# Reordering the last half block of a four-layer kernel: where the block ahead is finished, and who multiplies the last half's factors

## The chip, the cores and the metric

The kernel runs on one core of one Trainium2 chip. The metric is device time in microseconds (us) of one execution. A core has four computing engines, each with its own instruction queue worked in order: PE (TensorE, matrix products, results in PSUM), DVE (VectorE), ACT (ScalarE) and POOL (GpSimd); SP (SyncE) here only issues DMAs. Before the change three runs took 1389.89, 1390.21 and 1393.8 us, median 1390.21.

## What is computed

Eight stages one after the other on a residual x of 8 x 512 rows of 128 values in float32: for each of four layers an attention-like part and a feed-forward part, each behind a layer norm and added to x. The change touches the last one, in which both operands of every product are rounded to a 4-bit grid by blocks of 16:

```python
def fp4_quant_dequant(x):
    """Blockwise FP4 (E2M1) quantize + dequantize along the last dim."""
    shape = x.shape
    xb = x.reshape(shape[:-1] + (shape[-1] // BLOCK, BLOCK))
    scale = jnp.max(jnp.abs(xb), axis=-1, keepdims=True) / 6.0
    scale = jnp.maximum(scale, jnp.float32(1e-12))
    xn = xb / scale
    idx = jnp.searchsorted(_MID, jnp.abs(xn))
    q = _GRID[idx] * jnp.sign(xn) * scale
    return q.reshape(shape)
...
gate = fp4_linear(x, w_gate)
y = fp4_linear(x, w_up)
h = jax.nn.silu(gate) * y
return fp4_linear(h, w_down)
```

Here x has 128 columns and h has 352. fp4_linear rounds both operands so and multiplies them. The stage ahead of it in the same layer is a causal filter of 21 taps along the rows.

## The kernel before, in words

The eight batches of 512 rows ("blocks") go through the last two layers in frames: a loop over frames runs the attention of the layer before, and hooks in it call steps of the last layer for earlier blocks. The last frames have no attention left to hide behind. For them the function `end()` (line 2358) writes the order out by hand; the tile framework keeps it on each engine and sets the waits between engines from what each instruction reads and writes. Three things are interleaved there: **L**, the feed-forward of the block before the last (four tiles of 128 rows), and **A** and **B**, the two halves of the last block (two tiles each: 0 and 1, 2 and 3). The steps, with their lines:

- `quant_x1`, `quant_x2`, `turn_x` (2101): round the normalized x (VectorE, the last multiple on GpSimd), turn it on PE, copy it on ACT.
- `gated(j, at_end, thirds)` (2115) and `gate_out` (2127): two products of 352 columns (line 250, the helper of all products) into a pair of PSUM banks; tanh on ACT (2131). With `thirds` also a copy of the second product on ACT (2134). `gated_v` (2147) runs the rest: (tanh + 1) x gate on VectorE (2137), then the factor that makes h: with `thirds` on GpSimd, from SBUF (2139), else on VectorE, from PSUM (2141). Before the change L is called without `thirds`, A and B with.
- `quant_h1` (2154) calls `fp4_scale` (1363): maxima of the blocks of 16 (reduction, 1374), reciprocals (1376, 1377), scale (GpSimd, 1378), normalized values (1379). `quant_h2` calls `fp4_round` (1382): mask the exponent (1391), maximum and multiple (1394), add (1395), subtract (1396) on VectorE, then the multiple by the scale on GpSimd (1397), for two tiles at once (704 values a partition). `quant_h2_tile` (2160) does it for one tile (352).
- `turn_h` (2183): per tile three transposes on PE (2189) and a copy on ACT (2192). `down` (2196): three products a tile, then `added` (2072; line 2073), the sum into x on VectorE, and `stored` (2211; line 2212), the DMA of the result.
- `keep_clock(n)` (814): n products of the identity with itself, whose result nobody reads; they only keep PE working.

A float32 product of this kernel shows as two passes (records) in the trace, a transpose as one. PSUM banks named "one" go round in pairs: whoever takes the third waits until the first has been read. So B's first turned tile takes the bank of A's products. The buffers of the scale, of the normalized values and of the masks exist once for each size.

Of the kernel before, what the change touches and what calls it, by code (L numbers as in the profile page):

```python
# [17 lines left out]
F32 = mybir.dt.float32  # L18
I32 = mybir.dt.int32
U32 = mybir.dt.uint32  # L20
AF = mybir.ActivationFunctionType
ALU = mybir.AluOpType
# [3 lines left out]
P = 128  # L26
# [138 lines left out]
def body(ctx, tc, dram, spans, x_in, ib, it, ic, ei, out):  # L165
    nc = tc.nc
# [22 lines left out]
    def bank(tag="one"):  # L189
        if tag == "one" and "own" in banks:  # L190
            return banks["own"]
        return banks["pool"].tile([P, TB], F32, tag=tag, name="ps1", bufs=banks["tags"][tag])
# [5 lines left out]
    def load(blob, engine, pool=const):  # L198
        rows, cols = dram[blob].shape
        t = pool.tile([rows, cols], F32, tag=f"blob_{blob}", name=f"blob_{blob}")  # L200
        engine.dma_start(t, dram[blob])
        return {k: t[:, lo:hi] for k, (lo, hi) in spans[blob].items()}

    x = [resid.tile([P, J, D], F32, tag=f"x{b}", name=f"x{b}") for b in range(NB)]
    c = load("c", nc.scalar)
# [43 lines left out]
    def mm(out_, lhs, rhs, start=True, stop=True):  # L249
        nc.tensor.matmul(out_, lhs, rhs, start=start, stop=stop)  # L250
# [25 lines left out]
    def cols(t, j):  # L276
        return t[:, j * P : (j + 1) * P]
# [536 lines left out]
    def keep_clock(n):  # L814

        ps = bank()
        for _ in range(n):
            mm(cols(ps, 0), ident, ident)
# [563 lines left out]
    def fp4_round(pool, dst, sc, a, blocks, room=None):  # L1382

        shape = [P, blocks, 16]
        room = room or blocks
        m = pool.tile([P, room, 16], F32, tag=f"fm{room}", name="fm")[:, :blocks, :]  # L1390
        nc.vector.tensor_scalar(
            m.bitcast(I32), a.bitcast(I32), 0x7F800000, None, ALU.bitwise_and
        )
        nc.vector.tensor_scalar(m, m, 1.0, 1.5 * 2.0**22, ALU.max, ALU.mult)
        nc.vector.tensor_tensor(a, a, m, ALU.add)  # L1395
        nc.vector.tensor_tensor(a, a, m, ALU.subtract)
        nc.gpsimd.tensor_tensor(
            dst.rearrange("p (n k) -> p n k", k=16),
            a,
            sc.unsqueeze(2).to_broadcast(shape),  # L1400
            ALU.mult,
        )
# [3 lines left out]
    def late():  # L1406
# [11 lines left out]
        with tc.tile_pool(name="a2", bufs=2) as wp, tc.tile_pool(name="l3", bufs=1) as lp:  # L1418
# [253 lines left out]
            def context(n):  # L1672
                ex, sm, vs = exs.pop(n)
                ps = bank("c")
                for kt in range(J):
                    for i in range(2):
                        mm(
                            ps[64 * i : 64 * (i + 1), :],
                            vs[:, kt, i, :],
                            ex[kt][:, i, :],  # L1680
                            start=(kt == 0),
                            stop=(kt == J - 1),
                        )
                ct = wp.tile([P, TB], F32, tag="ct", name="ct")
                nc.scalar.copy(ct, ps)
                return ct

            def output(n, ct):
                b, cc = divmod(n, 8)
                if cc == 0:  # L1690
                    outs[b] = bank("o")
                for j in range(J):
                    mm(
                        cols(outs[b], j),
                        cols(ct, j),
                        cols(a2["l"], cc),
                        start=(cc == 0 and j == 0),
                        stop=(cc == 7 and j == J - 1),
                    )
                if cc == 7 and n < N - 1:  # L1700
                    add_to_residual(b, outs[b].rearrange("p (j d) -> p j d", j=J))
# [284 lines left out]
            def shared3(b):  # L1986

                t = {}

                def xp():  # L1990
                    if "xp" not in t:
                        t["xp"] = lp.tile([P, pad + TB], F32, tag="xp", name="xp", bufs=2)
                        nc.gpsimd.memset(t["xp"][:, :pad], 0.0)
                    return t["xp"]

                def tile_(name, make):
                    if name not in t:
                        t[name] = make()
                    return t[name]

                return xp, tile_

            def layer3(b, xp, tile_, part=(0, J), conv_bank="one", h_tag="h"):
# [4 lines left out]
                n = hi - lo  # L2008
# [63 lines left out]
                def added(ps):  # L2072
                    nc.vector.tensor_tensor(
                        x[b][:, j0:j1, :],
                        x[b][:, j0:j1, :],
                        ps[:, lo:hi].rearrange("p (j d) -> p j d", d=D),
                        ALU.add,
                    )
# [78 lines left out]
                def quant_h2(i):  # L2157
                    fp4_round(lp, pair(i), *t["fh", i], 44)

                def quant_h2_tile(i, j):  # L2160
                    sc, a = t["fh", i]
                    k = slice(22 * j, 22 * (j + 1))
                    h = tile_("h", h_tile)
                    fp4_round(lp, h[:, 2 * i + j, :], sc[:, k], a[:, k, :], 22)

                def blocks_h(i):
                    m = lp.tile([P, 44, 16], F32, tag="fm44", name="hb")
# [26 lines left out]
                        )  # L2194

                def down():
                    ht = tile_("ht", None)
                    po = bank()
                    for j in range(j0, j1):
                        for k, _ in thirds:  # L2200
                            mm(
                                cols(po, j),
                                ht[:C3, j, k, :],
                                wt["down"][:C3, k, :],
                                start=(j == j0 and k == 0),
                                stop=(j == j1 - 1 and k == 2),
                            )
                    added(po)
                    stored()

                def stored():
                    nc.sync.dma_start(
                        out[b * TB + lo : b * TB + hi, :].rearrange("(j p) d -> p j d", p=P),
                        x[b][:, j0:j1, :],
                    )
# [107 lines left out]
            for b in range(1, NB):  # L2323
                stats, scale, turn_, t_ = norm_steps(b, new_xt(b), "lb")
                n = {1: 3, 2: 5, 3: 14, 4: 26, 5: 33, 6: 40, 7: 47}[b]
# [32 lines left out]
            def end():  # L2358

                xp, tile_ = shared3(NB - 1)  # L2360
                A, B = (
                    layer3(NB - 1, xp, tile_, (2 * i, 2 * i + 2), "co"[i], "ge") for i in range(2)
                )
                L = last
                f = start[NB - 2]
                for key in [k for k in steps if k[0] >= f + 8]:
                    del steps[key]
                ct = context(N - 1)
                output(N - 1, ct)
                for h in (A, B):  # L2370
                    h.added(outs[NB - 1])
                    h.stats()
                L.gated(0, True, False)
                L.gated(1, True, False)
                A.scale()
                A.turn_()
                L.gated_v(0)
                B.scale()
                L.gated(2, True, False)
                L.gated_v(1)  # L2380
                B.turn_()
                L.gated(3, True, False)
                A.conv_tile(0)
                A.conv_tile(1)
                L.quant_h1(0)
                L.gated_v(2)
                L.quant_h2(0)
                L.gated_v(3)
                L.quant_h1(1)
                A.conv_added()  # L2390
                A.stats2()
                L.turn_h(0)
                L.quant_h2(1)
                B.conv_tile(2)
                B.conv_tile(3)
                A.scale2()
                A.quant_x1()
                A.quant_x2()
                B.conv_added()
                B.stats2()  # L2400
                A.turn_x()
                A.gated(0, True)
                B.scale2()
                A.gated(1, True)
                L.turn_h(1)
                A.gated_v(0)
                B.quant_x1()
                A.gated_v(1)
                B.quant_x2()
                L.down()  # L2410
                keep_clock(6)
                B.turn_x()
                B.gated(2, True)
                B.gated(3, True)
                A.quant_h1(0)
                A.quant_h2(0)
                B.gated_v(2)
                B.gated_v(3)
                keep_clock(8)
                B.quant_h1(1)  # L2420
                A.turn_h(0)
                B.quant_h2_tile(1, 0)
                B.quant_h2_tile(1, 1)
                A.down()
                keep_clock(22)
                B.turn_h(1)
                B.down()

# [290 lines left out]
```

## Time and profile before

| | us |
|---|---|
| median of three runs | 1390.21 |
| the profiled execution, its own time | 1394.63 |
| its span, first to last instruction | 1392.8 |
| L's sum into x (line 2073, 128x512) starts | 1369.92 |
| A's rounding: reduction starts / last subtraction starts | 1370.53 / 1375.10 |
| A's multiple on GpSimd (line 1397) starts | 1376.14 |
| B's gate factors on GpSimd (line 2139) | 1377.48 to 1379.29 |
| B's rounding: reduction starts / last subtraction starts | 1379.33 / 1385.51 |
| A's sum into x / B's sum into x start | 1385.95 / 1389.24 |
| last DMA issue (line 2212) starts | 1389.69 |

Times within the span count from the first instruction. Over the whole span PE is busy for 95%, DVE and ACT for 73% each, POOL for 46%; these shares say little about the last 30 us, which are read instruction by instruction. In a row of the timeline stand the start, the length, the engine, the line and the tiles written and read (`h<-fa,fsc`), and in brackets how long the engine had been idle and whose result ended that.

### The profile page before, as it was taken

To read this page: it belongs to the slowest core of one execution; us is meant where nothing else is said; L and a number is where in the kernel's file an instruction comes from. 1 tells how busy PE (TensorE), PEld (TensorE's weight loads), DVE (VectorE), ACT (ScalarE), POOL (GpSimd) and SP (SyncE) were. 2 spreads that over 40 slices of the span, in tenths; PEclk is the share of its full clock that TensorE was granted. 3 is DMA by queue.
4 is the path that set the end of the run, shared out by engine and by line. 5 is a ranking of instruction groups with operands and counts; after the bars stand their busy time and mean duration, and the time that the engine had idled before them with its cause. 6 is when DMAs were issued, how large, how long until landed. Compare 5 with 4: busy or idle time off the path is not lost.

```text
span 1392.8 us, 33124 instructions
## 1 busy us (share of the span) xinstructions
PE 1325.6 (95%) x12918; PEld 705.9 (51%) x12918; DVE 1013.9 (73%) x2149; ACT 1013.0 (73%) x2058; POOL 642.5 (46%) x749
## 2 busy tenths in 40 slices
PE   7889999999989999999999999999999999999997
PEld 3662222222267655547447545555555555555576
DVE  5786556666467778863783778888788797887876
ACT  6869999999978566665684686786767767667632
POOL 5655666666632533330472354353443634424432
PEclk9999999999999999999999999999999999999999
DMA  5019999999681011241211101101011010110000
GB/s 180 1 27 133 137 127 127 133 129 135 87 272 31 28 40 35 55 123 30 61 31 38 44 2 22 29 3 33 20 22 23 9 33 20 18 27 9 2 9 16
DMA packets 110845, 80.28 MB, mean 58 GB/s; under 512 B 61728, under 2 KB 103456, under 8 KB 106337
## 3 DMA queue, kind: packets, MB, share of 16 engines
q1 hardware_dynamic: 108959, 74.23, 29.0%
q0 software_dynamic: 1152, 2.36, 0.6%
q8 instruction: 102, 1.67, 0.5%
q10 hardware_dynamic: 578, 1.57, 0.3%
q14 instruction: 54, 0.44, 0.1%
HBM read 60.09 MB, written 18.04 MB: 56 GB/s over the span
## 4 chain that ended last, share of the span: by engine, by line
PE 50%; ACT 23%; DVE 20%; issue 3%; POOL 2%; DMA 1%; SPq 0%; DVEq 0%; ACTq 0%; POOLq 0%
PE ps L250 40%; PE ps L1571 8%; ACT hm L570 6%; ACT ex L1650 6%; DVE nm L1644 5%; ACT hm L569 3%; ACT prod L2038 2%; DVE acc L2024 1%; PE ps L2221 1%; DVE fa L1395 1%; DVE s L732 1%; DVE fa L1379 1%; ACT h L389 1%; DVE fsc L1374 1%; ACT q L1532 1%
## 5 line engine op out<-in xcount | busy, mean ns | idle before, releaser
L1650 ACT ACTIVATE ex<-ps,nm 128x512 f32<-128x512 f32 x512 | 345.2, 687 | 174.5 <-DVE nm L1644 166.2
L1644 DVE TENSOR_REDUCE nm<-ps 128x2 f32<-128x1024 f32 x256 | 301.1, 1210 | 39.2 <-PE ps L250 39.0
L250 PE MATMUL ps<-q,k 64*64 64x512 f32 (+1 forms) x2240 | 258.4, 564 | 9.1 <-ACT ex L1650 7.1
L250 PE MATMUL ps<-ex,vs 128*64 128x512 f32 x1024 | 233.8, 598 | 1.3 <-DVE sm L1664 1.1
L1665 POOL TENSOR_TENSOR vs<-v,sm 128x256 f32<-128x256 f32 x128 | 78.4, 613 | 294.4 <-DVE sm L1664 270.6
L588 POOL TENSOR_TENSOR acc<-acc,pr 128x512 f32<-128x512 f32 x119 | 165.5, 1391 | 93.8 <-DVE pr L582 85.8
L1571 PE MATMUL ps<-xt,blob_a 64*64 64x512 f32 x912 | 207.8, 589 | 0.1
L570 ACT ACTIVATE hm<-ps,blob_f 128x1536 f32<-128x1536 f32 x128 | 196.2, 1533 | 0.0
L582 DVE SCALAR_TENSOR_TENSOR pr<-ps,blob_f,gs 128x512 f32<-128x512 f32 x120 | 90.0, 750 | 93.6 <-PE ps L250 72.2
L250 PEld LDWEIGHTS ps<-q,k 64*64 64x64 f32 x2240 | 74.7, 132 | 152.4 <-ACT ex L1650 78.3
L250 PE MATMUL ps<-h,w 32*128 32x512 f32 x1024 | 147.4, 639 | 1.1 <-ACT hm L569 0.6
L250 PEld LDWEIGHTS ps<-ex,vs 128*64 128x64 f32 x1024 | 68.4, 136 | 152.9 <-issue 129.7
L250 PE MATMUL ps<-hm,w 128*32 128x512 f32 x1024 | 136.2, 604 | 3.8 <-DVE pr L582 3.1
L2039 POOL TENSOR_TENSOR acs<-acs,prod 128x512 f32<-128x512 f32 x96 | 124.1, 1292 | 24.2 <-ACT prod L2038 19.4
L1571 PE MATMUL ps<-blob_a,ct 64*64 64x128 f32 x1824 | 118.6, 269 | 0.0
L1571 PE MATMUL ps<-blob_a,xt 64*64 64x128 f32 x1824 | 118.5, 269 | 0.0
L1571 PEld LDWEIGHTS ps<-blob_a,ct 64*64 64x64 f32 x1824 | 106.2, 133 | 0.0
L1650 ACT ACTIVATION_READ_ACCUMULATOR ex<-ps,nm 128x1 f32 x512 | 105.0, 205 | 0.0
L1571 PEld LDWEIGHTS ps<-blob_a,xt 64*64 64x64 f32 x1824 | 103.0, 133 | 0.0
L569 ACT ACTIVATE hm<-ps,blob_f 128x512 f32<-128x512 f32 x128 | 88.0, 687 | 13.3 <-PE ps L250 13.2
L250 PEld LDWEIGHTS ps<-h,w 32*128 32x128 f32 x1024 | 40.7, 183 | 108.4 <-ACT hm L569 98.9
L1571 PEld LDWEIGHTS ps<-xt,blob_a 64*64 64x64 f32 x912 | 61.7, 132 | 31.9 <-issue 28.4
(368 smaller groups left out, 2204.1 us busy)
## 6 DMA issues: line engine op xcount, KB each, us to landing
gs<-gates SPq DMA_DIRECT2D x248, 128.0 KB, 7.5
ht<-turned_h SPq DMA_DIRECT2D x20, 180.0 KB, 3.0
turned_h<-hb SPq DMA_DIRECT2D x40, 88.0 KB, 2.3
blob_f<-in_f SPq DMA_DIRECT2D x1, 2560.0 KB
blob_a<-in_a SPq DMA_DIRECT2D x1, 2056.0 KB
x<-in_x SPq DMA_DIRECT2D x8, 256.0 KB, 5.1
gates<-turned SPq DMA_DIRECT2D x32, 64.0 KB, 4.8
slots_in<-nought SPq DMA_DIRECT2D x8, 256.0 KB, 4.4
```

The costliest lines, as they stand in the source:

```text
L250: nc.tensor.matmul(out_, lhs, rhs, start=start, stop=stop)
L389: nc.scalar.activation(hk, hk, AF.Sigmoid, bias=bi[:, k : k + 1], scale=sc[:, k : k + 1])
L569: nc.scalar.activation(hm[:, 0, :], p1, AF.Gelu, bias=bias)
L570: nc.scalar.activation(hm[:, 1:, :], p3, AF.Gelu, bias=bias)
L582: nc.vector.scalar_tensor_tensor(pr, po, f0["b2"][:, e : e + 1], gs, ALU.add, ALU.mult)
L588: nc.gpsimd.tensor_tensor(acc[:, b, :], acc[:, b, :], pr, ALU.add)
L1571: ins = nc.tensor.matmul(*args, **kw).ins
L1644: nc.vector.tensor_reduce(nm, ps, AX.X, ALU.max, negate=True)
L1650: nc.scalar.activation(ex[kt][:, i, :], ps[:, i, :], AF.Exp, bias=nm[:, i : i + 1], accum_out=sm[:, kt, i : i + 1],)
L1665: nc.gpsimd.tensor_tensor(vs[:, tiles, :, :], vs_[n][:, tiles, :].rearrange("p j (i n) -> p j i n", i=2), sm[:, tiles, :].unsqueeze(3).to_ ...
L2038: nc.scalar.activation(p, src, AF.Copy, scale=w)
L2039: nc.gpsimd.tensor_tensor(t["acs"], t["acs"], p, ALU.add)
```

## The change

It is all in `end()` and in the steps that it calls. L's `down` is cut in two: its products go behind the gates of B's tiles and into another bank ("c"), its sum and its store behind A's. B's gates are called without `thirds`. B's rounding of h masks both tiles at once and then goes tile by tile, with the multiple of the first tile on GpSimd and of the second on VectorE. The counts of `keep_clock` become 17, none, and 13, where they were 6, 8 and 22.

```diff
-                def quant_h2_tile(i, j):
+                def quant_h2_pair(i):
                     sc, a = t["fh", i]
-                    k = slice(22 * j, 22 * (j + 1))
-                    h = tile_("h", h_tile)
-                    fp4_round(lp, h[:, 2 * i + j, :], sc[:, k], a[:, k, :], 22)
+                    m = lp.tile([P, 44, 16], F32, tag="fm44", name="fm")
+                    nc.vector.tensor_scalar(
+                        m.bitcast(I32), a.bitcast(I32), 0x7F800000, None, ALU.bitwise_and
+                    )
+                    nc.vector.tensor_scalar(m, m, 1.0, 1.5 * 2.0**22, ALU.max, ALU.mult)
+                    for j, engine in enumerate((nc.gpsimd, nc.vector)):
+                        k = slice(22 * j, 22 * (j + 1))
+                        nc.vector.tensor_tensor(a[:, k, :], a[:, k, :], m[:, k, :], ALU.add)
+                        nc.vector.tensor_tensor(a[:, k, :], a[:, k, :], m[:, k, :], ALU.subtract)
+                        engine.tensor_tensor(
+                            tile_("h", h_tile)[:, 2 * i + j, :].rearrange("p (n k) -> p n k", k=16),
+                            a[:, k, :],
+                            sc[:, k].unsqueeze(2).to_broadcast([P, 22, 16]),
+                            ALU.mult,
+                        )
...
                 def down():
+                    down_out(down_products(bank()))
+
+                def down_products(po):
                     ht = tile_("ht", None)
-                    po = bank()
...
+                    return po
+
+                def down_out(po):
                     added(po)
                     stored()
...
                 B.quant_x2()
-                L.down()
-                keep_clock(6)
+                keep_clock(17)
                 B.turn_x()
-                B.gated(2, True)
-                B.gated(3, True)
+                B.gated(2, True, False)
+                B.gated(3, True, False)
                 A.quant_h1(0)
                 A.quant_h2(0)
                 B.gated_v(2)
                 B.gated_v(3)
-                keep_clock(8)
+                po = L.down_products(bank("c"))
                 B.quant_h1(1)
                 A.turn_h(0)
-                B.quant_h2_tile(1, 0)
-                B.quant_h2_tile(1, 1)
+                B.quant_h2_pair(1)
                 A.down()
-                keep_clock(22)
+                L.down_out(po)
+                keep_clock(13)
                 B.turn_h(1)
                 B.down()
```

## The prediction

> **What bounds the kernel now.** I read the page first (PE busy for 95% of the span, yet the chain that ended last gives ACT 23% and DVE 20%), then only the end, from 1362 us on, which is all that the edit touches: the chain of waits in order of time, the timeline, and the busy time by stretches. In the chain, columns are start, length, what:
>
> ```profile
> 1369.92 0.69 DVE x L2073
> 1370.61 0.81 DVE fsc L1374
> ...
> 1376.14 1.38 POOL h L1397
> 1377.52 1.78 POOL h L2139 x2
> 1379.30 0.02 issue
> 1379.33 0.90 DVE fsc L1374
> ...
> 1386.03 0.34 DVE x L2073
> 1386.38 0.14 issue
> 1386.51 0.53 PE ps L2189 x3
> ...
> 1389.24 0.42 DVE x L2073
> ```
>
> The end is VectorE's, from 1369.92 on. PE's products (line 250) stand in it only until 1369.90 and again at 1387.60. Three pieces are not arithmetic that the last half needs on VectorE just then: L's sum into x (0.69 us), the 3.16 us that the chain spends on GpSimd before VectorE's next reduction (A's rounding multiple, then B's two gate factors), and the last stretch, where B's transposes wait for A's sum into x.
>
> **The change, part by part** (times are of the profiled execution: span 1392.8 us, 1394.63 us in all; the median of the three runs is 1390.21, so I carry over differences only).
>
> 1. *L's sum leaves its place.* VectorE goes from B's rounding (its last subtraction ends at 1369.89) straight to A's reduction. Independent instructions there start 0.08 us before the one ahead ends (1369.92 + 0.69 against 1370.53), so the reduction starts at 1369.81, not 1370.53: **-0.72**. Its clock products: 34 passes stand where 24 + 12 stood, (1371.06 - 1366.94) / 36 = 0.114 us each, so B's turning starts 0.23 us earlier, at 1370.83, after its data (GpSimd ends at 1370.66). B's gates end by 1374.2; their tanh is long done when the factors come at 1375.2. The whole A rounding shifts by 0.72: its last subtraction ends at 1375.27, GpSimd's multiple of A runs 1375.42 to 1376.80.
>
> 2. *L's products after B's gates.* 24 passes at 0.116 (2.78 in 1366.94 to 1369.72) run from 1374.15 to 1376.93, about when A's h is ready (1376.86). So A's turning starts at 1376.95, not 1377.58, its products end by 1379.6, and A's sum needs them only at 1384: 4 us of cover. The bank "c" that they write was last read at 1352.07. Cost nothing; if the cover went, see the rivals.
>
> 3. *B's factors on VectorE.* Two ACT copies (0.46 each) go, off the path. In place of two 0.93 us products on GpSimd come two of line 2141 (0.52). The sequence of line 2137, 2141, 2137, 2141 as in L: 1375.19, 1375.73, 1376.17, 1376.71, ending 1377.23. The reduction (line 1374) starts at 1377.26: 1.99 after A's last subtraction where it was 3.34: **-1.35**. It also needs A's multiple to be done (its scale buffer exists once): 1376.80, 0.46 us of cover.
>
> 4. *B's rounding as a pair.* Up to the normalized values nothing changes (2.53 us): 1379.79. Then mask 0.56, maximum 0.56 (the 704-wide rows at 1373.05), add 0.56, subtract, add, subtract of 352 (0.53 and 0.52 each, the middle add 0.08 early): the last subtraction would end at 1382.99, 5.73 after the reduction, where before it took 6.70. But GpSimd's multiple of the first tile is asked for at 1382.15, beside those adds. What happens then, the trace shows elsewhere (start, length, engine, line):
>
> ```profile
> 711.65 1.66 DVE L2024 SCALAR_TENSOR_TENSOR acc<-xp,blob_l,acc 128x512 f32<-128x512 f32 x1
> ...
> 712.83 1.62 POOL L2039 TENSOR_TENSOR acs<-acs,prod 128x512 f32<-128x512 f32 x1
> 713.34 1.66 DVE L2024 SCALAR_TENSOR_TENSOR acc<-xp,blob_l,acc 128x512 f32<-128x512 f32 x1
> ...
> 738.64 0.61 POOL L1665 TENSOR_TENSOR vs<-v,sm 128x256 f32<-128x256 f32 x1
> 738.72 1.08 DVE L2070 TENSOR_TENSOR acc<-acc,acs 128x512 f32<-128x512 f32 x1 [0.41 <-POOL acs L2039]
> ```
>
> Line 2024 reads two tiles of SBUF and takes 0.75 alone, 1.66 here; line 2070 0.68 alone, 1.08 here: such an instruction stands still while GpSimd works, and GpSimd (1.28 alone) waits in its turn, by starts. So GpSimd begins when the second add ends (1382.44), takes 0.65 (as in before from 1384.07, when VectorE lets it in, to 1384.72), and the second subtraction ends 0.38 after it, 1383.47: 0.48 lost of 0.97, **-0.49**. The Trainium skill, SBUF — State Buffer, "Who interferes with whom", has this as a rule: an instruction with two SBUF inputs and a GpSimd one that reads SBUF exclude each other for their whole length, while one with a single SBUF input does not collide. Trace and rule agree; by a reading in which only constant-operand instructions collide (the 0.81 for 0.34 at 1384.11) the 0.48 would not be paid. Line 2141, with one input in PSUM, ran 0.52 at 1347.62 inside GpSimd's 1.39, so part 3 is free of it.
>
> 5. *The last tile's multiple on VectorE, and the tail.* Before, from last subtraction (1386.03) to B's sum (1389.24): 3.21. Now: multiple 0.53 (line 1395's 352-wide row; same width) from 1383.50 to 1384.03, A's sum 0.41, early by 0.08, to 1384.36; B's turning waits for that sum, since its bank is A's (0.15 later, as 1386.36 to 1386.51): 1384.51. To the first product 1.12 (1.09 and 1.16 in the two turnings before): 1385.63; to the sum 1.64: 1387.27. That is 3.80: **+0.59**. L's sum (0.69; its products are done since 1377) and its store lie inside the turning. On SP that store now comes behind A's and ahead of B's; its 256 KB took about 2.1 us from issue (1370.64 to 1372.7), so from some 1385.0 they land by 1387.2, before B's store (issue 1387.7, then 0.37). What follows B's sum is as before (landing, 1.3 us of closing).
>
> Sum: -0.72 - 1.35 - 0.49 + 0.59 = -1.97.
>
> 6. *The clock of PE in that tail.* Only 13 clock products stand where 22 did: PE is done at 1382.66 and idle to 1384.51, then again 0.25. The trace has one place where so little work was followed by half clock (us, PE busy, ..., PEclk):
>
> ```profile
> 382.32:385.73 3.41, 1.63 (x14) 0.50 (x11) 1.78 (x3) 3.38 (x7) 2.54 (x2) 1.00 0.00 0
> 385.73:389.15 3.42, 3.42 (x17) 3.34 (x16) 0.17 (x1) 0.26 (x1) 0.01 (x1) 0.50 0.00 0
> ...
> 399.39:402.80 3.41, 1.65 (x15) 1.44 (x14) 0.92 (x2) 3.38 (x8) 0.00 (x0) 1.00 0.97 357
> ...
> 1382.43:1385.84 3.41, 2.83 (x26) 2.64 (x24) 3.20 (x7) 0.00 (x0) 0.87 (x1) 1.00 0.00 0
> 1385.84:1389.25 3.41, 2.59 (x18) 2.02 (x18) 0.54 (x3) 0.95 (x2) 0.78 (x1) 1.00 0.13 38
> ```
>
> I cut the span by the 3.41 us of the half-clock piece, on from its start. A stretch with 1.63 us of PE work was followed by one at 0.50; one with 1.65 was not. The same grid puts the last drop at 1392.67, after a stretch with none. In before the stretch from 1382.43 has 2.83; now it has 0.23 + 0.87 + 0.21 = 1.31, so I take the clock to halve at 1385.84. A 128-wide pass costs 0.215 there (385.74 to 386.17 for two) for 0.116; some 10 of the last 12 passes lie behind it: **+1.0**. The bounds are 0 and +1.5 (all 12, and 0.3 on the transposes). One execution shows one phase of the grid; were it to differ in others, more than 1.78 us of idle time would fall into one stretch for (1386.39 - 1384.44) / 3.41 = 57% of phases. The Trainium skill, TensorE: Matmul & The Clock Gate, "Part 1: The HAM clock gate", gives a free-running window of 3413 ns and half rate after an idle one: the length agrees with the 3.41 here, but if idle means a whole empty window the clock would stay full and the sum would be -1.97; the 1.63 us of work ahead of the drop speak against that.
>
> **Forecast:** -1.97 + 1.0 = -0.95: 1393.7 for a profiled execution like this one, **1389.3** for the median.
>
> **Rivals.**
> - *The clock stays full.* For: 43% of phases, and 1.65 us of work was enough once. -1.97: 1388.2.
> - *No collision either* in part 4: against it the two rows at 711.65 and 738.72. -2.45 at full clock: 1387.8.
> - *Slower: B's factors wait for A's multiple.* Both write the tile h. If the two halves of h are not told apart, line 2141 at 1375.73 starts only after GpSimd ends at 1376.80: +1.09 on all that follows, and PE then idles 3 us, so the tail is wholly at half clock, +1.5: -1.97 + 1.09 + 1.5 = +0.6: 1390.8. Then the edit has put one wait on GpSimd in place of another; it decides from a wait of about half a microsecond. For it: the reduction at 1348.75 waits 0.61 for GpSimd. Against: at 1347.62 line 2141 wrote one half of h while line 1397 was writing the other, so what that reduction waited for was the scale buffer.
> - *PE becomes the bound:* if its clock halved from the gates at 1371.7 on, L's 24 passes (5.2) would end near 1382, A's products near 1387, and the tail at half clock (4.3 us from A's sum) would put B's sum at 1391.6, 2.4 late: 1392.6. It decides once PE is 4 us late; every stretch here shows clock 1.00.
>
> **Chances.** Forecast 0.42, full clock 0.30, no collision 0.07, factors waiting 0.08, PE bound 0.03, something unseen or scatter (the three runs span 3.9 us) 0.10. Range: from the case without collision, 0.4 lower for scatter, to the factors waiting: 1387.4 to 1390.9. A measurement of this kernel tells about 0.3%, 4.2 us, from no change; every case worked out lies within that, and the unseen I split evenly: faster 0.05, same 0.90, slower 0.05.
>
> **What would show it.** Right: A's reduction directly behind line 1396 without line 2073 between; the reduction of B's h some 1.99 us after A's last subtraction, released by VectorE itself; one 352-wide subtraction stretched to near 1.0 beside GpSimd's multiple; L's sum inside B's turning; PEclk 0.5 near the last products. Wrong: line 2141 released by GpSimd; B's transposes released by GpSimd; L's store landing after B's. If the gain is over 3 us, I have missed a stall that these steps do not name.

## The result, and the profile after

| | before | after |
|---|---|---|
| median of ten runs each, us | 1392.03 | 1388.18 |
| ratio, 95% interval | | 0.9971 (0.9961 to 0.9981) |
| profiled execution, own time / span | 1394.63 / 1392.8 | 1389.91 / 1388.1 |
| A's turned x copied by ACT (line 2106), start | 1362.32 | 1360.21 |
| B's sum into x, start | 1389.24 | 1384.54 |
| **last stretch**: from that copy to B's sum | **26.92** | **24.33** |

The time fell by 0.29%, some 4 us, just inside the 0.3% that count as no change here. The copy of A's turned x stands ahead of everything that the edit moves, in a part of the program that is the same in both kernels; that it starts 2.11 us earlier is therefore not the edit's doing by any step I can name. What the edit can have done lies in the last stretch: 2.59 us, where I had forecast 0.95. I measure every kernel below by that stretch, which repeats to 0.01 us.

The chain of waits of the kernel after, in order of time (start, length, what); the one of before stands in the prediction:

```profile
1367.36 0.43 DVE fa L1396
1367.79 0.81 DVE fsc L1374
...
1373.63 0.52 DVE h L2141
...
1375.25 0.90 DVE fsc L1374
...
1380.46 1.00 DVE fa L2170
...
1382.07 0.34 DVE x L2073
1382.41 0.04 issue
1382.46 0.54 PE ps L2201 x3
1383.00 1.52 PE ps L250 x12
...
1384.54 0.42 DVE x L2073
```

L's sum is gone from behind line 1396, A's reduction follows directly. GpSimd no longer stands ahead of B's reduction (1375.25): VectorE's own factors do (2137, 2141). And the end is new. In before the chain goes through the three transposes of B's first tile, ACT's copy of them and then twelve product passes; in after it goes through the three of the second tile and the twelve passes, of which the first six, the first tile's, run while ACT copies the second tile (1383.04 to 1383.52, beside the chain). The timeline of the same profile shows why (idle time and its releaser in brackets):

```profile
1379.90 0.52 DVE L2169 TENSOR_TENSOR fa<-fa,fm 128x352 f32<-128x352 f32 x1
1380.14 0.93 POOL L2171 TENSOR_TENSOR h<-fa,fsc 128x352 f32<-128x352 f32 x1 [3.27 <-DVE fa L2170]
1380.46 0.99 DVE L2170 TENSOR_TENSOR fa<-fa,fm 128x352 f32<-128x352 f32 x1
...
1381.12 0.55 PE L2201 MATMUL ps<-blob_c,h 128*120 128x128 f32 x3 [0.69 <-POOL h L2171]
...
1382.46 0.54 PE L2201 MATMUL ps<-blob_c,h 128*120 128x128 f32 x3 [0.79 <-DVE x L2073]
```

The first three lines are the collision that part 4 forecast: GpSimd asks at 1380.14, VectorE's second subtraction takes 0.99 for 0.53. The last two are what it missed: B's first tile is turned when GpSimd hands it over, at 1381.12, while only the second waits for A's sum. PE is thus never idle for long, and its clock stays at 1.00 to the last product.

### The profile page after: what moved, and what is told of

The parts are those of the page before. It is cut to its first block, busy times and chain, and to the rows that moved or that the text cites. A ratio compares the mean times of both kernels' runs of the same rounds, so it can differ in the third digit from the quotient of the medians.

```text
span 1388.1 us, 33098 instructions
## 1 busy us (share of the span) xinstructions
PE 1323.9 (95%) x12906; PEld 703.8 (51%) x12906; DVE 1015.7 (73%) x2150; ACT 1012.2 (73%) x2056; POOL 640.1 (46%) x746
## 3 DMA queue, kind: packets, MB, share of 16 engines
q8 instruction: 102, 1.67, 0.5%
## 4 chain that ended last, share of the span: by engine, by line
PE 52%; ACT 22%; DVE 20%; issue 3%; POOL 2%; DMA 1%; SPq 0%; DVEq 0%; ACTq 0%; POOLq 0%
PE ps L250 41%; PE ps L1571 8%; ACT hm L570 6%; ACT ex L1650 6%; DVE nm L1644 5%; ACT hm L569 3%; ACT prod L2038 2%; DVE acc L2024 1%; DVE s L732 1%; PE ps L2238 1%; DVE fa L1379 1%; DVE fa L1395 1%; DVE fsc L1374 1%; ACT h L389 1%; ACT q L1532 1%
## 5 line engine op out<-in xcount | busy, mean ns | idle before, releaser
L1571 PEld LDWEIGHTS ps<-blob_a,ct 64*64 64x64 f32 x1824 | 106.2, 133 | 0.0
```

Source lines behind the costliest of these rows:

```text
L1571: ins = nc.tensor.matmul(*args, **kw).ins
```

## The experiments

All numbers are the last stretch in us, from one profile each; expectations are quoted as they stood before the run.

### Is it the edit, or what lies ahead of it: before and after once more

> The kernel before once more, to see how much of the measured difference lies ahead of the edit. In the profiles of before and after the last stretch (from ACT's copy of A's turned x, line 2106, to the start of B's sum into x, line 2073) is 26.92 and 24.33 us, 2.59 apart, but that copy itself starts 2.11 us earlier in the profile after, in a part of the program that is the same in both. Theory: the edit is worth 2.6 us, and what the runs show beyond it is scatter upstream of it. Then this run's last stretch is 26.9 again, its span varies by up to 4 us, and the drift between its profile and the first one of before lies ahead of 1362 us. Rival: the edit itself makes the upstream part faster (layout of memory or instructions). Then this profile's copy starts near 1362.3 as in before, not near 1360.2.

> The kernel after once more. Theory (2.6 us from the edit, the rest scatter upstream): the last stretch is 24.3 us, and the difference of the medians is between 2 and 4.5 us. Rival (upstream part faster through the edit): the copy of A's turned x starts near 1360.2 again in every profile, and the difference is 4 us or more.

| kernel | copy of A's turned x starts | last stretch | median | ratio to 21 further runs of before (1394.52) |
|---|---|---|---|---|
| before, again | 1361.04 | 26.92 | 1393.35 | 0.9993 (0.9984 to 1.0002) |
| after, again | 1363.43 | 24.33 | 1391.78 | 0.9978 (0.9969 to 0.9987) |

The stretch repeats exactly. The copy does not: this time the kernel after reached it 2.39 us later than the kernel before, not earlier. Over all 14 profiles of this document the copy starts between 1360.2 and 1364.1, with kernels of both orders at either end. So the 2.11 us of the first pair were scatter ahead of the edit, and the rival that the edit sped up the rest falls. The differences of medians (1.6 against before again, 2.7 against the 21 further runs, 3.9 above) lie on both sides of the 2.59, the first of them below the expected 2 to 4.5; a program differs from itself by 0.07% here, 1 us, so whole times can't say it finer.

### The parts, one at a time

Each of these is the kernel before with one part of the edit.

```diff
 only_L
-                L.down()
-                keep_clock(6)
+                keep_clock(17)
...
-                keep_clock(8)
+                po = L.down_products(bank("c"))
...
                 A.down()
+                L.down_out(po)
 only_gates
-                B.gated(2, True)
-                B.gated(3, True)
+                B.gated(2, True, False)
+                B.gated(3, True, False)
 only_pair
-                B.quant_h2_tile(1, 0)
-                B.quant_h2_tile(1, 1)
+                B.quant_h2_pair(1)
```

> The kernel before with one part of the edit: L's products behind B's gates, its sum and store behind A's, clock products 17, none, 22. B's factors stay on GpSimd, the rounding goes tile by tile, and B's first turned tile takes the bank of A's products as in before. Expected from the prediction's first term: 26.92 - 0.72 = 26.2 us for the last stretch, L's store landing ahead of B's. Rival (what leaves VectorE only lengthens its wait for GpSimd): 26.9 us.

> The kernel before with one part of the edit: B's gate factors on VectorE. L's sum stays where it was, the rounding goes tile by tile. From the prediction's third term and its size in the profile after (1.26): 25.7 us for the last stretch; since B's first turned tile takes another bank than A's products here, up to 0.26 less, so 25.4 to 25.7 us. Rival (the reduction then waits for A's multiple on GpSimd instead): 26.4 us or more.

> The kernel before with one part of the edit: B's rounding as a pair, first tile's multiple on GpSimd, second's on VectorE. L's sum and B's factors stay, B's first turned tile takes the bank of A's products. From the prediction's fourth and fifth terms (-0.49 and +0.59): 27.0 us for the last stretch, that is, this part alone gains nothing. Rival (the pair gains by itself what the sum of parts lacks, about half a microsecond): 26.3 us.

Measured: only_L **26.21** (-0.71; expected 26.2), only_gates **25.82** (-1.10; expected 25.4 to 25.7), only_pair **27.04** (+0.12; expected 27.0). In only_L B's reduction comes 0.71 earlier: its wait for GpSimd did not grow, and that rival falls. The rival of the factors waiting for A's multiple falls too: in only_gates line 2141 ran inside GpSimd's multiple, which writes the other half of the same tile:

```profile
1374.20 1.39 POOL L1397 TENSOR_TENSOR h<-fa,fsc 128x704 f32<-128x704 f32 x1 [4.07 <-DVE fa L1396]
1374.51 0.52 DVE L2141 SCALAR_TENSOR_TENSOR h<-s,ps 128x352 f32<-128x352 f32 x1
...
1378.25 5.08 PE L250 MATMUL ps<-blob_c 128*128 128x128 f32 x44
...
1382.75 0.41 DVE L2073 TENSOR_TENSOR x<-x,ps 128x256 f32<-128x256 f32 x1
...
1383.47 0.84 PE L2189 MATMUL ps<-blob_c,h 128*120 128x128 f32 x6
```

What only_gates misses is PE's doing: its 22 clock products last to 1383.33, and B's turning starts behind them, all six transposes together, at 1383.47. That is 0.16 later than 0.15 behind A's sum (line 2073, 1382.75 to 1383.16), the distance in before, and it leaves nothing of what the other bank could give, which the first tile has here (in the trace its transposes wait for semaphores of GpSimd and PE; in before for those of GpSimd and VectorE). The three parts together make -1.69, and the whole makes -2.59. Nine tenths of a microsecond belong to none of them.

### The missing part: one clock product

The count of clock products ahead of B's turning was the one number of the diff that I had read only for the clock.

```diff
 keep_16 (the kernel after; 17 in keep_17)
-                keep_clock(13)
+                keep_clock(16)
```

> The kernel after with 16 clock products ahead of B's turning in place of 13. Which PSUM bank B's first turned tile takes depends on this count: with 16 it is the bank of the clock products, as in the kernel after. PE is then done at about 1381.07 on the clock of the profile after, when GpSimd hands over the first tile. Both theories: last stretch 24.3 to 24.4 us.

> The kernel after with 17 clock products, one more than in keep_16, so that PE works 0.23 us longer. From this count on B's first turned tile takes the bank of A's products and has to wait for A's sum into x. Theory (the bank was the step that the prediction had wrong, worth 0.7 us): the six transposes start together some 0.15 us after A's sum, and the last stretch is 25.1 us. Rival (the tail is shorter for another reason, say because L's products left the banks in the middle): 24.4 to 24.6 us.

keep_16 **24.34**, keep_17 **25.06**: 0.72 us for one clock product of 0.23. The timelines, first keep_16, where the two turned tiles start apart:

```profile
1384.04 0.52 PE L2201 MATMUL ps<-blob_c,h 128*120 128x128 f32 x3
...
1385.24 0.54 PE L2201 MATMUL ps<-blob_c,h 128*120 128x128 f32 x3 [0.69 <-DVE x L2073]
```

then keep_17, where all six transposes wait for A's sum, and the products for ACT's copy behind them:

```profile
1384.22 0.84 PE L2201 MATMUL ps<-blob_c,h 128*120 128x128 f32 x6 [1.22 <-DVE x L2073]
...
1385.30 1.60 PE L250 MATMUL ps<-wd,ht 120*128 120x128 f32 x12 [0.24 <-ACT ht L2204]
```

In the traces of after, keep_0 and keep_16 (13, none and 16 clock products) the first tile's transposes do not wait for VectorE's semaphore; in keep_17 they do. The count alone does not decide it: with 22 they wait for VectorE in before and not in only_gates. So the tile framework does not hand out the two "one" banks strictly in turn, as I had assumed; which rule it follows (a model of its own of when each bank comes free would fit) is not shown here. The closure is good: the parts' -1.69, and 0.16 that PE's clock products took from only_gates (25.82 against 26.92 - 1.26 = 25.66, with 1.26 the shift of the last subtraction there), make -1.85; keep_17, the whole edit with the waiting bank, is at -1.86.

### The bank alone, in the kernel before

```diff
 bank_before
-                A.down()
+                A.down_out(A.down_products(bank("o")))
```

> The kernel before with one thing changed: A's products go into the bank o, which is free by then, so that none of B's turned tiles waits for A's sum into x. GpSimd then hands over the second tile at the same moment as in before, some 0.9 us after the last subtraction, and that sets the copy of the second tile. Theory (the bank wait costs as much as the work behind it lets it: 0.7 us where VectorE makes the second tile, less here): the first tile is turned ahead of the last subtraction's end, its products run earlier, and the last stretch is 0.2 to 0.3 us shorter, 26.6 to 26.7 us. Rival (the bank alone is worth 0.7 us in any kernel): 26.2 us.

```profile
1384.14 0.49 PE L2189 MATMUL ps<-blob_c,h 128*120 128x128 f32 x3
1384.55 0.52 DVE L1396 TENSOR_TENSOR fa<-fa,fm 128x352 f32<-128x352 f32 x1
...
1385.15 0.79 POOL L1397 TENSOR_TENSOR h<-fa,fsc 128x352 f32<-128x352 f32 x1 [1.40 <-DVE fa L1396]
...
1385.99 0.54 PE L2189 MATMUL ps<-blob_c,h 128*120 128x128 f32 x3 [1.36 <-POOL h L1397]
```

**26.71**, 0.21 off. The first tile is turned early (1384.14), but GpSimd hands over the second one (its multiple started 0.08 after VectorE's last subtraction) at the same time as ever, and that is what the end waits for. The wait for the bank costs 0.7 us only where nothing else holds the second tile: it needs the edit's other parts.

### The clock

```diff
 keep_0 (the kernel after)
-                keep_clock(13)
```

> The kernel after without the 13 clock products ahead of B's turning; the banks stay as they are. PE is then idle for 3.7 us before the first transposes and works 0.55 us of the next 1.3. Theory (a stretch of 3.41 us with at most some 1.63 us of work is followed by half clock; the kernel after escaped it since its idle time there is only 0.7 and 0.8 us): the granted clock is 0.5 for most of the last products, and the last stretch is 24.9 to 25.8 us. Rival (clock products do nothing this close to the end): 24.3 us at clock 1.00.

**25.87**, 1.54 more than after, a little above what I expected. Busy time by stretches of 3.41 us (us, then busy time and count of PE, PEld, DVE, ACT, POOL, then PEclk, DMA share, GB/s):

```profile
1380.56:1383.97 3.41, 0.58 (x6) 0.39 (x4) 3.27 (x6) 0.00 (x0) 0.24 (x1) 1.00 0.00 0
1383.97:1387.38 3.41, 2.09 (x9) 1.69 (x10) 2.49 (x5) 0.74 (x2) 0.69 (x1) 0.50 0.12 36
1387.38:1390.80 3.42, 2.26 (x11) 1.96 (x10) 0.42 (x1) 0.21 (x1) 0.00 (x0) 0.50 0.27 80
```

A stretch with 0.58 us of work, and the next is at half clock, as is the one behind it: the transposes and all twelve passes (2.76 us for 1.67) lie in the two. So half clock this close to the end can happen, and the 1.54 is near the upper bound of 1.5 in part 6; this is one execution. In the profile of after it did not fall due; its stretches, cut by its own half-clock piece, carry 2.0 us of work each:

```profile
1378.97:1382.39 3.42, 2.01 (x17) 1.57 (x15) 3.25 (x7) 0.48 (x1) 0.93 (x1) 1.00 0.00 0
1382.39:1385.80 3.41, 2.05 (x15) 1.77 (x15) 1.03 (x3) 0.48 (x1) 0.00 (x0) 1.00 0.38 115
```

### The collision

```diff
 both_vector (the kernel after)
-                    for j, engine in enumerate((nc.gpsimd, nc.vector)):
+                    for j, engine in enumerate((nc.vector, nc.vector)):
```

> The kernel after with both tiles' multiples by the scale on VectorE, none on GpSimd. The second subtraction then has no GpSimd instruction beside it. Theory (the 0.99 us that it takes in the profile after, for 0.53, is VectorE held by GpSimd): it takes 0.53, and the time saved pays for the multiple that VectorE does in addition: last stretch 24.3 to 24.4 us. Rival (it is long for another reason, as a wait on the instruction ahead): it stays near 1.0 and the last stretch is 24.8 us.

```profile
1382.11 0.52 DVE L2169 TENSOR_TENSOR fa<-fa,fm 128x352 f32<-128x352 f32 x1
...
1384.29 0.52 DVE L2170 TENSOR_TENSOR fa<-fa,fm 128x352 f32<-128x352 f32 x1
...
1384.85 0.53 DVE L2171 TENSOR_TENSOR h<-fa,fsc 128x352 f32<-128x352 f32 x1
...
1385.52 0.51 PE L2201 MATMUL ps<-blob_c,h 128*120 128x128 f32 x3 [1.03 <-DVE h L2171]
```

The subtraction takes 0.52 with nothing on GpSimd beside it: the 0.99 was the collision. **24.15**, better than either expectation: the time saved pays for the added multiple but for 0.15 (last subtraction 21.39 after the copy, 21.24 in after), and the second turned tile, which got another bank here, starts 0.14 behind the multiple instead of waiting for A's sum, 0.38 behind it.

The prediction's other reading, that only constant-operand instructions collide, falls with this. But its "Trace and rule agree" goes too far the other way, since it tells the rule without a condition. The Trainium skill, SBUF — State Buffer, "Who interferes with whom", says that an instruction with at most one SBUF input does not collide with GpSimd outside the modes that use two ports. The trace of before has a one-input instruction that is held: line 1394 reads one tile, takes 0.34 alone (1382.23) and 0.81 beside GpSimd.

```profile
1383.85 0.87 POOL L1397 TENSOR_TENSOR h<-fa,fsc 128x352 f32<-128x352 f32 x1 [2.90 <-DVE fa L1396]
1384.11 0.81 DVE L1394 TENSOR_SCALAR fm<-fm 128x352 f32<-128x352 f32 x1
```

The reduction of line 1374, with one input too, was not held (0.88 at 1367.71 in after, beside GpSimd from 1367.93). No run here shows in which mode either of them works.

### A's sum out of the way, and a version meant to beat both

```diff
 sum_inside (the kernel after)
                         nc.vector.tensor_tensor(a[:, k, :], a[:, k, :], m[:, k, :], ALU.add)
+                        if j:
+                            meanwhile()
                         nc.vector.tensor_tensor(a[:, k, :], a[:, k, :], m[:, k, :], ALU.subtract)
...
-                B.quant_h2_pair(1)
-                A.down()
+                pa = A.down_products(bank())
+                B.quant_h2_pair(1, lambda: A.down_out(pa))
 interleaved (the kernel after)
-                    for j, engine in enumerate((nc.gpsimd, nc.vector)):
-                        k = slice(22 * j, 22 * (j + 1))
...
+                    for op, by in ((ALU.add, m), (ALU.subtract, m), (ALU.mult, None)):
+                        for j in range(2):
+                            k = slice(22 * j, 22 * (j + 1))
...
+                            nc.vector.tensor_tensor(
+                                to,
+                                a[:, k, :],
+                                by[:, k, :] if by is not None else sc[:, k].unsqueeze(2).to_broadcast([P, 22, 16]),
+                                op,
+                            )
...
-                A.down()
+                A.down_out(A.down_products(bank("o")))
```

> The kernel after with A's sum into x moved on VectorE from behind the second tile's multiple to between the second add and the second subtraction, where VectorE stands still for GpSimd. The sum reads one tile of SBUF and one of PSUM, so it should not be held. B's second turned tile then waits for the second multiple alone. Expected: 0.33 us off, last stretch 24.0 us, and a whole time that can't be told from the kernel after. Rival (the sum is held by GpSimd as well, or it delays the second subtraction): 24.3 to 24.7 us.

> A version meant to beat both: the kernel after with the two tiles' adds, subtractions and multiples all on VectorE and taken in turn (add, add, subtract, subtract, multiply, multiply), so that no instruction stands behind one whose result it needs and none stands beside GpSimd, and with A's products in the bank o, so that no turned tile waits for A's sum. An independent instruction there starts 0.44 us after the one ahead, a dependent one 0.56: the second multiple ends about 2.73 us after the first add starts, where it takes 3.17 in the profile after, and the second turned tile waits for it alone. Expected: last stretch 23.8 to 23.95 us, some 0.45 us less than after; the whole time about 3 us below before. Rival (the first tile's later multiple, and with it its copy, becomes the bound): 24.1 to 24.3 us.

```profile
1384.02 0.93 POOL L2173 TENSOR_TENSOR h<-fa,fsc 128x352 f32<-128x352 f32 x1 [3.26 <-DVE fa L2172]
1384.22 0.41 DVE L2073 TENSOR_TENSOR x<-x,ps 128x256 f32<-128x256 f32 x1
1384.55 0.77 DVE L2172 TENSOR_TENSOR fa<-fa,fm 128x352 f32<-128x352 f32 x1
```

sum_inside **24.07** (expected 24.0): A's sum takes its 0.41 beside GpSimd's multiple, unheld, and the second subtraction ends where it did. interleaved **23.82** (expected 23.8 to 23.95), 0.51 less than after:

```profile
1380.68 1.83 DVE L2173 TENSOR_TENSOR fa<-fa,fm 128x352 f32<-128x352 f32 x4
1382.43 0.95 DVE L2173 TENSOR_TENSOR h<-fa,fsc 128x352 f32<-128x352 f32 x2
1383.10 0.95 PE L2203 MATMUL ps<-blob_c,h 128*120 128x128 f32 x6 [0.88 <-DVE h L2173]
...
1383.65 0.91 ACT L2206 COPY ht<-ps 120x384 f32<-120x384 f32 x2 [5.61 <-PE ps L2203]
...
1384.18 1.60 PE L250 MATMUL ps<-wd,ht 120*128 120x128 f32 x12
```

Six instructions in 2.70 us (1380.68 to 1383.38), from the first add to the end of the second multiple, against 3.18 in after (1378.90 to 1382.08), where GpSimd did one of the six and held another. What the order alone gives is seen against both_vector, which does the same six on VectorE chain by chain: 3.27 (1382.11 to 1385.38). Of these 0.57 only 0.33 reach the last stretch (24.15 to 23.82), because what the rival named is there, if not at its price: the first tile's copy (from 1383.65) now comes late, and all twelve passes stand behind it, from 1384.18 on. In whole times sum_inside is at 0.9981 (0.9970 to 0.9992) of before and interleaved at 0.9980 (0.9969 to 0.9991). Both intervals lie below before, by 0.2%, less than the 0.3% up to which no change is called here; neither is told apart from after, so that interleaved beats after is shown in the last stretch alone.

## Why the prediction was right, and where it was wrong

The median, 1388.18, lies in the range and 1.1 below the 1389.3; the direction and "within 0.3%" came true, the latter narrowly. That the absolute time came so near is partly luck. The forecast went from a median of 1390.21, three runs; ten runs of before gave 1392.03. Against that the medians fell by 3.85, four times the 0.95 forecast, and the last stretch by 2.59, nearly three times. The full-clock rival's 1388.2 is met by the same accident. By steps, in the last stretch:

| step | forecast | measured |
|---|---|---|
| 1, L's sum leaves its place | -0.72 | -0.71 (start of A's reduction) |
| 3, B's factors on VectorE | -1.35 | -1.26 (start of B's reduction) |
| 4, B's rounding, with the collision | -0.49 | -0.50 (end of the last subtraction) |
| 5, the multiple on VectorE, and the tail | +0.59 | -0.12 |
| 6, the clock of PE | +1.0 | 0 |
| sum | -0.95 | -2.59 |

Steps 1 to 4 hold to 0.1 us. Step 2's cover held: L's products ran from 1372.04 on, and A's turning followed directly at 1374.76. In step 3 most of the 0.09 that lack are, as I read the chain, one wait more: B's reduction now needs VectorE and GpSimd both, and its queue takes that in two pieces (0.10 between 1375.15 and 1375.25, where most steps show 0.02); no run tests this.

**Step 5 failed in one sentence:** "B's turning waits for that sum, since its bank is A's". I had taken that from the profile before, where it was so, and from banks going round in pairs. In the kernel after the first tile has the other bank and is turned when GpSimd hands it over, so that only the second tile's work stands behind A's sum. keep_16 and keep_17 put a price of 0.72 on it, the 0.71 that the step is off. The prediction had named the sign of this: "B's transposes released by GpSimd".

**Step 6 followed step 5 down.** Its idle time (1382.66 to 1384.51) was the wait for that bank. Without it PE has two gaps of 0.7 and 0.8 us and 2.0 us of work in each stretch. That the wait would have brought half clock is not shown: no run has the waiting bank together with 13 clock products (keep_17 has 17, and its last products ran at full clock). Its rule, half clock behind a stretch with less than about 1.65 us of work, fits keep_0, but does not cover all drops, as the last section shows.

Of the rivals, "the clock stays full" is what happened, but not for the reason given there (a lucky phase); "no collision" and "factors wait" fell by both_vector and only_gates; "PE becomes the bound" did not come near. The sign "the gain is over 3 us" came up in the medians (3.85), but not in the last stretch. In the profiles what goes beyond 2.59 us lies ahead of the edit, and it changes sign between the two pairs. Where it comes from was not pursued.

## What to carry to other kernels

A bank that a tile takes is part of the schedule: when an edit changes what stands between two users of a pool, look up in the built program which earlier user the later one waits for, and don't carry it over from the profile before. On VectorE, order independent halves in turn rather than chain by chain (2.70 us for 3.27 here), and keep a GpSimd multiple away from a two-input VectorE instruction that the end waits for (0.99 us for 0.53). When an edit is worth 0.2% of a long kernel, measure it from a fixed instruction ahead of it to the end of the chain: that repeated to 0.01 us where the whole time moved by 4.

## What the runs showed of the hardware that I had not expected

The half-clock piece of 3.41 us is not bound to a place in the program. Before and after-again have it at 385.7, after at 392.5, before-again at 391.1, keep_17 at 500.7, both_vector at 106.2 and 802.6. Cutting each of the 14 profiles by its own pieces, 12 of the 14 stretches between 25 and 1385 us with 1.64 us of PE work or less were followed by half clock. But 11 of the 23 drops in that range came behind stretches with 2.26 to 3.02 us of work, as in keep_17, of which the stretches before and during are:

```profile
497.25:500.66 3.41, 2.44 (x20) 2.04 (x18) 3.19 (x11) 1.47 (x4) 1.86 (x3) 1.00 0.05 19
500.66:504.08 3.42, 2.96 (x4) 1.17 (x4) 1.82 (x4) 0.00 (x0) 2.08 (x2) 0.50 0.33 106
```

So little busy time, as the profile counts it, is a good sign of a drop to come, but about half of the drops come without it. What sets those stays open.

GpSimd went in between two instructions of VectorE that follow each other within 0.04 us. In after GpSimd had asked at 1380.14 and VectorE's add ended at 1380.42; the subtraction issued at 1380.46 ended only at 1381.45, 0.38 behind the end of GpSimd's multiple (1381.07), so it lost 0.46 of its 0.99 us there.
